# Two of six chunks of the last shared feed-forward as products of exact parts, and the last half chunk placed around the slot turns

## The chip, the cores and the metric

The kernel runs on one core of a Trainium2 chip. A core has five engines with queues of their own: TensorE (PE in the profile, its weight loads PEld), VectorE (DVE), ScalarE (ACT), GpSimd (POOL) and SyncE (SP), which issues most of the DMA transfers. [...] The metric is the device time of one execution in microseconds (us).

## What is computed

Four layers of a gated transformer: each adds a cross attention to a context and a feed-forward, both scaled by the tanh of a gate. There are 2 x 256 = 512 tokens of width 256. Only the last feed-forward matters here: a mixture of eight experts, of which each token takes two, plus a shared network that every token passes.

```python
def _shared_mlp(x_flat, shared_w_up_gate, shared_w_down):
    gu = jnp.einsum('td,dm->tm', x_flat, shared_w_up_gate)
    gate, up = jnp.split(gu, [J], axis=-1)                      # J = 704
    return jnp.einsum('tm,md->td', jax.nn.silu(gate) * up, shared_w_down)
...
logits = jnp.einsum('td,de->te', x_flat, router)                # 8 experts
topk_logits, sel = jax.lax.top_k(logits, K)                     # K = 2
...                                                             # rows go to slots of their experts
return (routed + shared).reshape(b, s, d)
```

## The kernel before

The 512 tokens stand turned in `xT` (128 rows, 2 batches, 2 halves k of the width, 256 tokens). The shared way up is done by the generator `hidden` (line 304). Its 704 columns are cut into `JCH`: chunks 0 to 4 of 128 columns, chunk 5 of 64. For each chunk two results, `pa` for the gate and `pb` for the linear half, are accumulated in PSUM over k = 0, 1, as f32 products with the weights `sh` as the stationary operand; ACT takes silu of `pa`, DVE multiplies by `pb` into `hS`. `by_batch` does chunks 0 and 1 one batch at a time (256 columns), and 2, 3 and 4 over all 512. Chunk 5 has gate and linear columns in one product (`both_w`), and with `parts=True` the generator pauses between its two products, k = 0 and k = 1. Wherever `pause(ci, b)` says so, `hidden` yields, and the caller puts other work in between.

What stands around it in the text of the last layer:

- `choose3`, `twice3`, `places` and `send3` are the routing of one half of the tokens (`halves[0]`, `halves[1]`): the two best experts, the slot numbers `goes`, and four scatters by POOL of rows into the table `xg` in HBM (helper `scatter`, line 1855). The function `between` starts the first half's routing after chunk 0; the second half's follows the first pause.
- SP reads `xg` back in five loads `xg_sb` (line 1932), once all eight scatters have landed.
- `l3_slots(g)` turns a load on PE (four transposes into a PSUM tile `tr`) and lets ACT or DVE, in alternation, copy it to `xgT`. `pair_up` is the routed way up for two groups of 128 slots, `pair_turn` turns the hidden rows (two `tr` tiles), `pair_down` goes down and scatters to `yg`. A loop over five pairs interleaves them.
- Lines 1981 to 1988 are small DVE operations on `off`, a check of the data; PE sums it over the partitions in the product `good` (line 1990).
- `kept` (lines 1913 to 1919) holds the experts' weights; POOL makes `spread` from it.

How order comes about: a scheduler places the instructions on each engine when the program is built; of those whose inputs are ready in its own model of time it takes the one that is first in the text. `inline` (line 222) chains operations by hand in the order of the text: with `pe_line` all products of this part, with `line` the DVE operations of the routing, until `line.clear()`. `behind(i, j)` puts i after j on the same engine. Once built, each engine runs its order and waits at whatever is not ready.

Buffers go round by tag: PSUM has four of `mm`, two of `tr`, two of `acc`; SBUF has eleven of `q4` and fifteen of `q2`. A tile waits for the readers of the one that held its buffer before.

The kernel has a second way to multiply, from the second layer on. `cut` (line 594) clears the low 12 bits of a float. A value is then top + low, both exact in 12 bits, and `three` (line 639) makes the product of six instructions in the type float32r: top by top and low (scaled by 2^12) by low into one PSUM tile `same`, and a third kind, of differences, into `cross`. `joined` (line 648) puts the two together: one ACT operation and one scalar_tensor_tensor on DVE.

Of the kernel before, what the change touches and what calls it, by code (L numbers as in the profile page):

```python
# [17 lines left out]
F32 = mybir.dt.float32  # L18
F32R = mybir.dt.float32r
I32 = mybir.dt.int32  # L20
U8 = mybir.dt.uint8
AF = mybir.ActivationFunctionType
ALU = mybir.AluOpType
AX = mybir.AxisListType

P = 128
NT = 4
D = 256
T = NT * P
B = 2  # L30
# [9 lines left out]
EPS = 2.0 ** -12  # L40
# [10 lines left out]
def flamingo(ctx: ExitStack, tc: tile.TileContext, a: dict, out: bass.AP):  # L51
    nc = tc.nc
# [6 lines left out]
    q4 = pool("q4", Q4)  # L59
    q2 = pool("q2", Q2)  # L60
# [7 lines left out]
    nat = pool("nat", 1)  # L68
# [35 lines left out]
    def pair(i, name, dtype=F32):  # L104
        return slab.tile([P, 2, WCOLS], dtype, tag=f"p{i}", name=name)

    def load(half, name):
        rows, cols = a[name].shape
        nc.sync.dma_start(half[0:rows, 0:cols], a[name])
        return half[0:rows, 0:cols]  # L110
# [83 lines left out]
    def behind(i, j, reason):  # L194

        tc.add_manual_dep(i.ins, j.ins.name, mybir.DependencyInfo(
            mybir.DependencyClass.NoSync, mybir.DependencyReason.DATA), reason=reason)
# [24 lines left out]
    def inline(i, line=line):  # L222
        if line:
            if line[-1] is not None:
                behind(i, line[-1], "in the order of the text")
            line[:] = [i]
        return i
# [35 lines left out]
    def batch(t, k, ts=slice(0, T)):  # L263
        return t[:, ts.start // 256 : ts.stop // 256, k, :]
# [14 lines left out]
    def mm(shape=None):  # L279
        return ps_mm.tile(shape or [P, 512], F32, tag="mm", name="mm")  # L280
# [20 lines left out]
        t = small.tile([P, 1], F32, tag="warm", name="warm", bufs=1)  # L301
        behind(nc.scalar.activation(t, eps_ln, fn), last, why)

    def hidden(xT, chunks, act_w, lin_w, hT, both_w=None, pause=lambda ci, b: False, parts=False):


        ps = {}
        for ci, (off, sz), ts in by_batch(chunks):
            if sz == 64:
                if parts:  # L310
                    p = ps_acc.tile([P, T], F32, tag="acc", name="both")
                    for k in range(2):
                        inline(nc.tensor.matmul(p, lhsT=both_w(k), rhs=batch(xT, k), start=(k == 0), stop=(k == 1)), pe_line)
                        if k == 0:
                            yield
                else:
                    p = mm()
                    chain(p, [(both_w(k), batch(xT, k)) for k in range(2)])
                s = q2.tile([P, T], F32, tag="q2", name="silu")
                nc.scalar.activation(s[64:], p[:64], AF.Silu)  # L320
                nc.vector.tensor_mul(hT[ci // 2][64:, ci % 2, :], s[64:], p[64:])
                continue
            if ci not in ps:
                ps[ci] = mm(), mm()
            pa, pb = ps[ci]
            for w, p in ((act_w, pa), (lin_w, pb)):
                chain(p[:sz, ts], [(w(k, off, sz), batch(xT, k, ts)) for k in range(2)])
            if ts.stop == T:
                s = q2.tile([P, T], F32, tag="q2", name="silu")
                silus[:] = [nc.scalar.activation(s[:sz, :], pa[:sz, :], AF.Silu)]  # L330
                nc.vector.tensor_mul(hT[ci // 2][:sz, ci % 2, :], s[:sz, :], pb[:sz, :])
            if pause(ci, ts.stop // T):
                yield
# [260 lines left out]
    def cut(dst, src):  # L594

        return nc.vector.tensor_scalar(dst.bitcast(I32), src.bitcast(I32), -4096, None, ALU.bitwise_and)
# [43 lines left out]
    def three(same, cross, left, right):  # L640

        for k in range(2):
            for i in range(2):
                inline(nc.tensor.matmul(same, lhsT=left(i, k), rhs=right(i, k), start=(k == 0 and i == 0), stop=(k == 1 and i == 1)), pe_line)  # L644
        for k in range(2):
            inline(nc.tensor.matmul(cross, lhsT=left(2, k), rhs=right(2, k), start=(k == 0), stop=(k == 1)), pe_line)  # L646

    def joined(dst, same, cross, scale=1.0):
        nc.scalar.mul(dst, cross, -EPS * scale)  # L649
        return inline(nc.vector.scalar_tensor_tensor(dst, same, (1.0 + EPS) * scale, dst, ALU.mult, ALU.add))  # L650
# [358 lines left out]
    t = totals.pop((15, 1))  # L1009
# [368 lines left out]
    def places(place, first, hot, s):  # L1378

        n = s.start  # L1380
        terms = [(s, ones_r, first[:, s]), (s, before, hot[:, s])]
        if n:
            terms += [(s, ones_r, hot[:, 0:2]), (s, ones_r, hot[:, 1:3])]
        terms += [(slice(n + 1, n + 2), ones_r, hot[:, 0:1])]
        for i, (to, lhsT, rhs) in enumerate(terms):
            inline(nc.tensor.matmul(place[:, to, :], lhsT=lhsT, rhs=rhs, start=(i == 0), stop=(i == len(terms) - 1)), pe_line)
# [269 lines left out]
    def halves_of(i, name):  # L1656
        w = pair(i, name)
        return [w[:, k, :] for k in range(2)]
# [5 lines left out]
    for q in range(QUADS + 1):  # L1664
        if q < QUADS:
            h = l2_up(q)
        if q == 0:
            second_rows()
        if 1 <= q <= QUADS:
            backs[q - 1] = l2_mask(q - 1)  # L1670
            acc = l2_down(q - 1, hTs.pop(q - 1))
            if q != 5:
                os[q - 1] = l2_halves(q - 1, acc)

        if q == 5:
            dn3 = [load(half, f"l3_dn{k}") for k, half in enumerate(halves_of(5, "dn3"))]
            sh = [load(half, f"l3_sh{k}") for k, half in enumerate(halves_of(0, "sh3"))]
            gu3 = [load(half, f"l3_gu{k}") for k, half in enumerate(halves_of(3, "gu3") + halves_of(4, "gu3"))]
        if q < QUADS:
            hTs[q] = l2_turn(q, h)  # L1680
        if q == 5:
            os[q - 1] = l2_halves(q - 1, acc)
        if 2 <= q < QUADS:
            homeward([(q - 2, 0)])
        if q == 5:
            homeward([(0, 1), (1, 1)])
        if q == QUADS:
            homeward([(4, 0), (2, 1), (3, 1), (4, 1)])
            load_table(AF.Exp, silus[0], "the table of exponentials")
# [105 lines left out]
    def l3_turned2(n):  # L1795
        tr = ps_tr.tile([P, 2, P], F32, tag="tr", name="tr")
        for k in range(2):
            inline(nc.tensor.transpose(tr[:, k, :], ext[2 * n][:, k * P : (k + 1) * P], ident), pe_line)
        nc.scalar.copy(tokens(xT, n), tr)
# [41 lines left out]
    def choose3(s):  # L1841
        for n in range(s.start, s.stop):
            inline(nc.vector.max(top[:, n, :], lgt[:, n, :]))
        inline(nc.vector.tensor_tensor(sel[:, s], lgt[:, s], wide(top[:, s, 1], 2), ALU.is_ge))

    def twice3(s):
        inline(nc.vector.tensor_tensor(hots[:, 0, s], lgt[:, s], wide(top[:, s, 0], 2), ALU.is_equal))
        inline(nc.vector.tensor_sub(hots[:, 1, s], sel[:, s].bitcast(F32), hots[:, 0, s]))
        t = small.tile([P, 2, 2], F32, tag="tie3", name="tie3", bufs=2)
        inline(nc.vector.tensor_tensor(t, top[:, s, 0:2], top[:, s, 1:3], ALU.is_equal))  # L1850
        inline(nc.vector.reduce_max(astray[:, s], t, axis=AX.X))
# [14 lines left out]
    def send3(s):  # L1866
# [10 lines left out]
                scatter(xg, goes[:, k, n : n + 1], ext[2 * n + k], E * CAP - 1, sent)  # L1877
        return i

    choose3(halves[0])  # L1880
    l3_rows(3)
    twice3(halves[0])

    def between(ci, b):
        if (ci, b) == (0, 0):
            places(place, base3, sel, halves[0])
            send3(halves[0])
            for n in (2, 3):
                l3_turned2(n)
        if (ci, b) == (1, 0):  # L1890
            for n in (2, 3):
                l3_logits(n)
        return (ci, b) in ((0, 1), (4, 1))

    shared = hidden(xT, JCH, lambda k, o, s: sh[k][:, o : o + s], lambda k, o, s: sh[k][:, 640 + o : 640 + o + s], hS,
                    lambda k: sh[k][:, 1280:], between, True)
    next(shared)
    choose3(halves[1])
    twice3(halves[1])
    places(place, base3, sel, halves[1])  # L1900
    routed = send3(halves[1])

# [5 lines left out]
    inline(nc.vector.tensor_reduce(clear3, astray, AX.X, ALU.max))  # L1908
    inline(nc.vector.tensor_scalar(clear3, clear3, -1.0, 1.0, ALU.mult, ALU.add))
    line.clear()  # L1910
    next(shared)
    kept = const.tile([P, 2, NT], F32, name="kept")
    nc.vector.tensor_scalar(w[:, 0, :], w[:, 1, :], -0.5, 0.5, ALU.mult, ALU.add)
# [89 lines left out]

    hs, hTs = {}, {}
    turn[0] = 1
    for g in range(2):
        l3_slots(g)
    next(shared)
    hs[0] = pair_up(0)
    for p in range(5):  # L2010
        if p < 4:
            hs[p + 1] = pair_up(p + 1)
        if p + 2 < 5:
            l3_slots(p + 2)
        if p == 0:
            for _ in shared:
                pass
        if 0 < p < 4:
            pair_down(p - 1)
        pair_turn(p)  # L2020
# [692 lines left out]
```

## Time and profile before

| | |
|---|---|
| median of 3 runs | 546.32 us (545.76 to 546.65) |
| the profiled execution | 545.36 us, of which the span 543.5 us |
| granted TensorE clock | 0.998 |
| PE busy | 535.0 us, 98% of the span |
| DVE, ACT, POOL busy | 61%, 44%, 23% |
| chain that ended last | PE 94%, DVE 3%, ACT 1% |
| between 485.29 and 498.25 us: PE, DVE, ACT busy | 12.96, 5.37, 2.64 us |

The span runs from the first to the last instruction of the execution; what the device time has beyond it lies around the program. Times below are counted from the span's start. A profile row names the engine, the line of the kernel, which can be a helper's (L284 is `chain`, L644 and L646 are `three`), the operation with output and input tiles, and in brackets how long the engine had stood still before and for whom. The chain of work that ended last is followed back from the last instruction: at each step to what released it, or to the one before it on its engine.

The last row is the sum of three neighbouring stretches of the shared way up, asked for one by one (485.29 to 487.85, to 491.3 and to 494.75, to 498.25): PE is full, the other engines are busy less than half of the time.

### The profile page before, as it was taken

How to read it: one execution, taken by the hardware profiler on the slowest of the kernel's cores; microseconds unless marked ns; L12 is line 12 of the kernel's file. 1: busy time of each engine (PE TensorE's matmuls, PEld its weight loads, DVE VectorE, ACT ScalarE, POOL GpSimd, SP SyncE). 2: the span in 40 equal slices, each digit the busy share in tenths (PEclk: the TensorE clock that was granted, in tenths of full speed). 3: DMA queues.
4: the chain of work that ended last, by engine and by line, in shares of the span. 5: the costliest groups of instructions: out<-in, count | busy, mean ns of one | idle time of the engine just before them, and what ended most of it. 6: DMA issues, size and time to landing. Idle time of an engine off the chain costs nothing.

```text
span 543.5 us, 8726 instructions
## 1 busy us (share of the span) xinstructions
PE 535.0 (98%) x3304; PEld 395.4 (73%) x3304; DVE 332.3 (61%) x777; ACT 238.1 (44%) x488; POOL 124.7 (23%) x229
## 2 busy tenths in 40 slices
PE   8999999999999999999999999999999999999996
PEld 6554775878888888887888888687776447884465
DVE  6999797745556454754547567765467536562322
ACT  6886466644354434444444533451433212422320
POOL 5776104111031110311012223112022001252150
PEclk9999999999999999999999999999999999999999
DMA  8910120000004000040000404599030799614013
GB/s 289 427 45 0 30 125 1 1 1 0 1 0 153 2 2 1 1 154 1 0 1 1 156 1 156 232 300 390 27 143 13 279 411 244 246 40 129 19 46 132
DMA packets 15528, 57.06 MB, mean 105 GB/s; under 512 B 2653, under 2 KB 5924, under 8 KB 12102
## 3 DMA queue, kind: packets, MB, share of 16 engines
q1 hardware_dynamic: 13718, 51.61, 25.9%
q0 software_dynamic: 1472, 4.28, 2.3%
q8 instruction: 28, 0.46, 0.3%
q10 hardware_dynamic: 288, 0.52, 0.3%
q14 instruction: 22, 0.18, 0.1%
HBM read 51.60 MB, written 5.25 MB: 105 GB/s over the span
## 4 chain that ended last, share of the span: by engine, by line
PE 94%; DVE 3%; ACT 1%; issue 0%; POOL 0%
PE mm L284 27%; PE acc L284 20%; PE mm L644 9%; PE mm L646 4%; PE mm L1590 4%; PE s L464 3%; PE acc L476 2%; PE q L644 2%; PE mm L1951 2%; PE acc L1616 2%; PE gu L644 2%; PE outT L721 1%; PE acc L1973 1%; PE q L646 1%; PE mm L1414 1%; PE y L1647 1%
## 5 line engine op out<-in xcount | busy, mean ns | idle before, releaser
L284 PE MATMUL mm<-qT,kT 128*128 128x256 f32 x256 | 60.7, 381 | 0.0
L284 PE MATMUL acc<-e,v 128*128 128x256 f32 x256 | 60.6, 379 | 0.0
L284 PEld LDWEIGHTS mm<-qT,kT 128*128 128x128 f32 x256 | 48.1, 190 | 9.2 <-ACT oT L836 1.6
L284 PEld LDWEIGHTS acc<-e,v 128*128 128x128 f32 x256 | 48.3, 189 | 8.2 <-issue 0.4
L632 POOL TENSOR_TENSOR h_parts<-w,h_top 128x256 fp32r<-128x256 f32 x28 | 20.8, 742 | 139.2 <-PE acc L284 73.6
L825 ACT ACTIVATE e<-mm 128x512 f32<-128x512 f32 x64 | 38.1, 598 | 22.3 <-PE mm L284 22.1
L828 DVE TENSOR_TENSOR t<-e,e 128x512 f32<-128x512 f32 x32 | 22.1, 691 | 23.6 <-ACT e L825 23.4
L468 ACT ACTIVATE e<-s 128x512 f32<-128x512 f32 x64 | 32.9, 605 | 5.5 <-PE s L464 5.4
L236 POOL TENSOR_TENSOR rstd<-mv,eps_ln 128x1 f32<-128x1 f32 x31 | 6.7, 217 | 108.8 <-DVE mv L235 108.8
L649 ACT ACTIVATE v<-mm 128x512 f32<-128x512 f32 x24 | 14.3, 597 | 31.1 <-PE mm L646 31.1
L644 PE MATMUL mm<-ctx_top,h_parts 128*128 128x512 f32 x56 | 27.3, 488 | 0.0
L284 PE MATMUL acc<-w,oT 128*128 128x256 f32 x112 | 26.8, 381 | 0.1
L836 ACT COPY oT<-acc 128x256 f32<-128x256 f32 x32 | 11.9, 372 | 34.2 <-PE acc L284 34.2
L650 DVE SCALAR_TENSOR_TENSOR v<-mm,v 128x512 f32<-128x512 f32 x24 | 16.6, 692 | 16.6 <-ACT v L649 16.6
L649 ACT ACTIVATE kT<-mm 128x512 f32<-128x512 f32 x28 | 16.7, 598 | 20.5 <-PE mm L646 20.5
L287 DVE SCALAR_TENSOR_TENSOR x<-acc,gsum,x 128x256 f32<-128x256 f32 x56 | 23.6, 477 | 2.8 <-PE acc L284 2.2
L650 DVE SCALAR_TENSOR_TENSOR kT<-mm,kT 128x512 f32<-128x512 f32 x28 | 19.3, 689 | 6.7 <-ACT kT L649 6.7
L284 PEld LDWEIGHTS acc<-w,oT 128*128 128x128 f32 x112 | 20.1, 190 | 3.5 <-ACT oT L836 0.5
L644 PE MATMUL mm<-v_parts,ctx_top 128*128 128x512 f32 x48 | 22.1, 461 | 0.0
L644 PE MATMUL mm<-ctx_rest,h_parts 128*128 128x512 f32 x56 | 22.0, 393 | 0.0
L464 PE MATMUL s<-w_q,ctx_nat 32*128 32x256 f32 x256 | 21.1, 400 | 0.2 <-ACT e L468 0.2
L650 DVE SCALAR_TENSOR_TENSOR qT<-q,qT 128x512 f32<-128x512 f32 x14 | 9.7, 692 | 18.4 <-ACT qT L649 18.4
(444 smaller groups left out, 1182.0 us busy)
## 6 DMA issues: line engine op xcount, KB each, us to landing
gu<-in_l_gu_all SPq DMA_DIRECT2D x14, 1024.0 KB, 7.6
w<-in_l_all SPq DMA_DIRECT2D x4, 2048.0 KB, 8.6
dn<-in_l_dn_all SPq DMA_DIRECT2D x4, 1024.0 KB, 6.2
dn<-in_l_dn_all SPq DMA_DIRECT2D x6, 512.0 KB, 9.3
gu<-in_l_gu SPq DMA_DIRECT2D x4, 704.0 KB, 18.6
ctxT<-in_ctxT SPq DMA_DIRECT2D x4, 512.0 KB, 10.9
ctx_nat<-in_ctx SPq DMA_DIRECT2D x3, 512.0 KB, 7.2
dn<-in_l_dn SPq DMA_DIRECT2D x2, 704.0 KB
```

Source lines behind the costliest of these rows:

```text
L284: inline(nc.tensor.matmul(dst, lhsT=lhsT, rhs=rhs, start=(i == 0), stop=(i == len(pairs) - 1)), pe_line)
L287: return inline(nc.vector.scalar_tensor_tensor(x[:, n, cols], acc, scalar, x[:, n, cols], ALU.mult, ALU.add))
L464: in_turn(nc.tensor.matmul(ps[j][:, k, :], lhsT=ctx_nat[rows, b, hf, c * P : (c + 1) * P], rhs=qm[rows, n, i, :], start=True, stop=True))
L468: exps.append(nc.scalar.activation(es[j], ps[j], AF.Exp))
L632: nc.gpsimd.tensor_sub(dst[1], src, t)
L644: inline(nc.tensor.matmul(same, lhsT=left(i, k), rhs=right(i, k), start=(k == 0 and i == 0), stop=(k == 1 and i == 1)), pe_line)
L646: inline(nc.tensor.matmul(cross, lhsT=left(2, k), rhs=right(2, k), start=(k == 0), stop=(k == 1)), pe_line)
L649: nc.scalar.mul(dst, cross, -EPS * scale)
L650: return inline(nc.vector.scalar_tensor_tensor(dst, same, (1.0 + EPS) * scale, dst, ALU.mult, ALU.add))
L825: nc.scalar.activation(e, s, AF.Exp)
L828: nc.vector.tensor_add(t, es[0], es[1])
L1590: inline(nc.tensor.matmul(ps[j * BLK : (j + 1) * BLK, :], lhsT=xsT[k][:, block * BLK : (block + 1) * BLK], rhs=gu2[home(q, j)][:, at : at ...
```

## The change

Chunks 3 and 4 of the shared way up are no longer f32 products. For them `hidden` calls `shared_by_parts`: for gate and linear half it runs `three` into an `mm` tile and a `tr` tile, then `joined`, then silu and the product into `hS`. The parts of the weights are made by `shared_weight_parts` (chunk 3's inside `between`, after the first half's scatters; chunk 4's after the second half's), the parts of x by `shared_x_top`, `shared_x_rest` and `shared_x_diff`, all on DVE with casts on ACT. There is one more pause, after chunk 1's second batch, and behind it the text has the parts. The parts live in buffers that held the context (`nat`, `ctxT`) and in two of `q4`. The two loads of `sh` go into one tile, by the same two transfers.

Chunk 5's first product now comes before the turns of slots 0 and 1, the second right after them; before, the first came after those turns and the second in the loop, after the turns of slots 2.

```diff
-    def hidden(xT, chunks, act_w, lin_w, hT, both_w=None, pause=lambda ci, b: False, parts=False):
+    def hidden(xT, chunks, act_w, lin_w, hT, both_w=None, pause=lambda ci, b: False, parts=False, by_parts=None, parted_chunks=()):
...
+            if ci in parted_chunks:
+                by_parts(ci, hT[ci // 2][:, ci % 2, :])
+                if pause(ci, ts.stop // T):
+                    yield
                 continue
...
-            sh = [load(half, f"l3_sh{k}") for k, half in enumerate(halves_of(0, "sh3"))]
+            sh_both = pair(0, "sh3")
+            sh = [load(sh_both[:, k, :], f"l3_sh{k}") for k in range(2)]
...
+    sx_two = nat.tile([P, 2, B, 2, 256], F32R, tag="nat", name="sx")
+    sx = [sx_two[:, 0], sx_two[:, 1], q4.tile([P, B, 2, 256], F32R, tag="q4", name="sx_diff")]
+    sw_four = turned_ctx.tile([P, 4, 2, 2, P], F32R, tag="ctxT", name="sw")
+    sw_two = q4.tile([P, 2, 2, 2, P], F32R, tag="q4", name="sw_two")
+    sw = {3: [sw_four[:, i] for i in range(3)], 4: [sw_four[:, 3], sw_two[:, 0], sw_two[:, 1]]}
+    x_tops = [q2.tile([P, 2, 256], F32, tag="q2", name="sx_top") for _ in range(B)]
+
+    def shared_weight_parts(ci):
+        w = sw[ci]
+        src = sh_both[:, :, 0:1280].rearrange("p k (j c) -> p k j c", j=2)[:, :, :, ci * P : (ci + 1) * P]
+        t = q2.tile([P, 2, 2, P], F32, tag="q2", name="sw_top")
+        inline(cut(t, src))
+        nc.scalar.copy(w[0], t)
+        inline(nc.vector.tensor_sub(w[1], src, t))
+        return lambda: inline(nc.vector.scalar_tensor_tensor(w[2], w[1].bitcast(F32), -1.0 / EPS, t, ALU.mult, ALU.add))
+
+    def shared_x_top(b):
+        i = inline(cut(x_tops[b], xT[:, b]))
+        if b:
+            behind(i, routed, "not among the routing")
+        nc.scalar.copy(sx[0][:, b], x_tops[b])
+
+    def shared_x_rest(b):
+        low = q2.tile([P, 2, 256], F32, tag="q2", name="sx_low")
+        behind(inline(nc.vector.tensor_sub(low, xT[:, b], x_tops[b])), routed, "not among the routing")
+        nc.scalar.mul(sx[1][:, b], low, 1.0 / EPS)
+
+    def shared_x_diff(b):
+        inline(nc.vector.tensor_sub(sx[2][:, b], x_tops[b], sx[1][:, b].bitcast(F32)))
+
+    def shared_by_parts(ci, dst):
+        sums = []
+        for j in range(2):
+            same, cross = mm(), ps_tr.tile([P, T], F32, tag="tr", name="cross3")
+            three(same, cross, lambda i, k: sw[ci][i][:, k, j, :], lambda i, k: batch(sx[i], k))
+            o = q2.tile([P, T], F32, tag="q2", name="shared3")
+            joined(o, same, cross)
+            sums.append(o)
+        nc.scalar.activation(sums[0], sums[0], AF.Silu)
+        nc.vector.tensor_mul(dst, sums[0], sums[1])
...
             send3(halves[0])
             for n in (2, 3):
                 l3_turned2(n)
+            shared_weight_parts(3)()
...
-        return (ci, b) in ((0, 1), (4, 1))
+        return (ci, b) in ((0, 1), (1, 1), (4, 1))
...
     twice3(halves[1])
+    shared_x_top(0)
     places(place, base3, sel, halves[1])
     routed = send3(halves[1])
...
     line.clear()
+    next(shared)
+    shared_x_rest(0)
+    shared_x_top(1)
+    shared_x_rest(1)
+    for b in range(B):
+        shared_x_diff(b)
+    shared_weight_parts(4)()
     next(shared)
...
+    next(shared)
     for g in range(2):
         l3_slots(g)
-    next(shared)
+    for _ in shared:
+        pass
     hs[0] = pair_up(0)
     for p in range(5):
...
-        if p == 0:
-            for _ in shared:
-                pass
```

More of the change, by code (lines that the diff above doesn't have):

```diff
@@ L321, in hidden @@
                 nc.vector.tensor_mul(hT[ci // 2][64:, ci % 2, :], s[64:], p[64:])
+                continue
+            if ci in parted_chunks:
+                by_parts(ci, hT[ci // 2][:, ci % 2, :])
+                if pause(ci, ts.stop // T):
+                    yield
                 continue
@@ L1892, in between @@
                 l3_logits(n)
-        return (ci, b) in ((0, 1), (4, 1))
+        return (ci, b) in ((0, 1), (1, 1), (4, 1))
     shared = hidden(xT, JCH, lambda k, o, s: sh[k][:, o : o + s], lambda k, o, s: sh[k][:, 640 + o : 640 + o + s], hS,
-                    lambda k: sh[k][:, 1280:], between, True)
+                    lambda k: sh[k][:, 1280:], between, True, shared_by_parts, (3, 4))
     next(shared)
```

## The prediction, made blind

> **What bounds the kernel now.** I read the page first: PE is busy 98% of the span at a granted clock of 0.998, and PE carries 94% of the chain that ended last. So I went to that chain for the last layer, where the change sits. Its columns are start, length (us) and what ran.
>
> ```profile
> 486.12 12.13 PE mm L284 x32
> 498.25 0.12 PE mm L1990 x2
> 498.37 0.93 PE tr L1940 x8
> 499.30 0.86 PE both L313 x2
> 500.16 4.87 PE mm L1951 x64
> 505.03 0.59 PE tr L1940 x4
> 505.62 0.86 PE both L313 x2
> 506.48 0.44 PE tr L1962 x4
> 506.92 2.50 PE mm L1951 x32
> ```
>
> Each piece starts where the one above ends: PE never pauses. The 12.13 us are the rest of chunk 1 and chunks 2, 3, 4 of the shared way up. L1990 is the small product `good`, L1940 the slot turns, the two L313 pieces the halves of chunk 5, L1951 the routed way up, L1962 its turns. The chain then stays on PE to 538.23; the gathered rows and their additions follow from the same PE products through POOL's scatters, so a shift at 500 us should reach the end whole.
>
> The price of the new kind of product is in the chain of the second layer, which already uses it:
>
> ```profile
> 113.12 0.94 PE mm L644 x4
> 114.06 0.46 PE mm L646 x2
> 114.51 1.73 PE mm L284 x8
> ```
>
> The six single-pass products of one 512-wide result take 0.94 + 0.46 = 1.40 us, most often 1.39 in this stretch.
>
> **The change, part by part.** *Chunks 3 and 4 on PE.* An f32 product is recorded as two instructions: the groups show 24 of 512 columns for the 12 products of chunks 2 to 4. The 12.13 us hold these and 8 of 256, that is 24 + 4 = 28 units of 0.433. Both outputs of a chunk take 8 units, 3.47 us. By parts: 2 x 1.39 = 2.78. Saved 0.69 a chunk, **1.37 us** for two; PE then ends chunk 4 at 496.88, if its parts are there.
>
> *The halves of chunk 5.* Work is moved, none is saved: 0.86 us go ahead of the slot turns, 0.86 from behind the third pair of slots to behind the first two. Turns start at 496.88 + 0.12 + 0.86 = 497.86. The first two slot loads are issued at 494.12 and 494.7 and land 2.7 and 2.9 us later (their rows), at 496.8 and 497.6; the second is wanted at 498.33. So they are in time by 1.0 and 0.7 us. Without the half ahead, the turns would have met them.
>
> But the half taken from 505.62 was a cover:
>
> ```profile
> 505.65 0.59 ACT L206 COPY xgT<-tr 128x512 f32<-128x512 f32 x1 [0.18 <-PE tr L1940]
> ```
>
> The third slots' turns end at 505.62 and ACT copies them out until 506.24. There are two `tr` buffers: the first hidden turn takes the free one (0.22 us), the second must wait for this copy, and so must the next way up, which reads xgT. Before, 0.86 us of chunk 5 lay there. Now the second turn can start 0.62 + about 0.05 us (478.09 to 478.13 in the chain is such a handover) after the slots' end instead of 0.22: PE stands **0.45 us**. In later turns `pair_down` (1.86 us) still covers.
>
> *Parts of chunk 3's weights.* DVE cut, subtraction, scalar_tensor_tensor, and one ACT cast. From the second layer's rows: cuts 0.42 us, subtractions 0.69, such casts on ACT 0.62. Back to back, DVE operations start closer than they last:
>
> ```profile
> 90.04 0.69 DVE L615 TENSOR_TENSOR ctx_w<-ctxT,ctx_w 128x512 f32<-128x512 f32 x1
> 90.65 0.76 DVE L596 TENSOR_SCALAR w_top<-w 128x512 int32<-128x512 int32 x2
> ```
>
> 0.61 for a 512-wide two-input operation, 0.34 for a cut. They stand in the routing's written order between 481.86 (first `goes`) and 483.87 (top of the second half), where DVE waited 2.01 us: 0.34 + 2 x 0.61 and two dependences are about 1.8. If they overrun by up to 0.9 us, PE's `places` (485.31) still hides it. Cost 0. The first half's cut of x falls into 484.89 to 485.77, also idle: 0. DVE's cost here is bounded by 0 and 0.3.
>
> *Parts of x and of chunk 4's weights* come behind the second `goes` (487.39): subtraction, cut, subtraction, two differences, then cut, subtraction, scalar_tensor_tensor: 6 x 0.61 + 2 x 0.34 = 4.3 us of DVE, plus hS of chunks 1 and 2. In the order of the text, x's parts are ready near 491.1 and the last difference near 492.0; chunk 3 starts on PE at 491.3 and wants the difference after four products, at 492.2. Chunk 4 (494.1) needs its weight parts (about 492.5) and the PSUM pair of chunk 2, which hS frees about 493.1. Slack 0.2, 0.2, 1.6 and 1.0 us: cost 0, with up to 0.5 if an operation slips in front. ACT gains 10 operations of 0.6 us in 16 us where it was mostly waiting; the four joins cost DVE 4 x 0.61.
>
> *`good` on PE* stays behind chunk 4 and needs DVE's `off` chain (L1981 to L1988), which ran until 489.98. These eight operations are last in the text. They take DVE 0.33 + 0.33 and six of 0.07, about 1.1 us, where others fill the gaps that each leaves to the next, and about 1.7 alone. Between 487.46 and 496.88, 9.4 us, DVE has 12 operations of 0.61 (hS of chunks 1 to 3, six for parts, three joins) and two cuts: 8.0 us. That leaves 1.4 us, and the joins wait for PE and ACT, so gaps are certain. I take 0; the other end is rival (b).
>
> *Joins and slot turns.* Cross results use the two `tr` buffers: the first slots' turns need the first one of chunk 4 (read by about 496.4), the second slots' the last (PE ends at 496.88, ACT reads it for 0.6: about 497.7, wanted at 498.33). ACT's copy of the first slots then stands behind chunk 4's silu and ends near 499.0; the way up wants it at 498.79 + 0.86 = 499.65, where the second half of chunk 5 hides it. Cost 0; without that half it would be some 0.3. POOL's spread moves behind a later `kept`; POOL has nothing else until 511.78.
>
> *Scatters.* The last of eight ends at 492.47 and paces the slot loads. The Trainium skill speaks against the change here (SBUF — State Buffer, Who interferes with whom): a tensor_scalar in two-port mode shuts GpSimd out for its whole length, so descriptors can't be written. The cuts (0.42 against 0.69 for the same width) look like that mode, and two fall among the last four scatters. The trace's nearest rows: scatters last 0.97 us whether or not a DVE operation runs (hS, 488.06), but none of those is a cut. By the row the loads keep their time, cost 0; by the rule, each cut delays by up to 0.42, together 0.84 against the 0.7 us of slack: PE would wait 0.14, and up to 0.7 if the first batch's two cuts delay it too. I take 0.
>
> The other edits cost nothing: one tile for `sh` instead of the same pair through a helper is the same two loads; reused context buffers were last read by 477.5. No DMA is added.
>
> **Sum.** -1.37 + 0.45 = **-0.92 us**. The profiled execution took 545.36 us (span 543.5 and 1.86 around); its sum is 544.44. It lies 0.96 below the median of the three runs, 546.32, from which I forecast **545.4**.
>
> **Rivals.** (a) *The stand at the third slots does not appear*, as the handover is hidden in the array's pipeline: the full 1.37, 545.0. For: durations of matmuls in the profile overlap by some 0.16 us; against: two separate dependences hang on the same copy.
>
> (b) *`good` becomes the new wait (slower).* The order on DVE is fixed when the program is built, by readiness and text order. If all of `off` falls behind hS of chunk 4, this is its time: the last join can't start before 497.7 (PE 496.88, ACT 0.6, handovers), so it ends at 498.4, hS at 499.1, and `off` alone takes 1.7, to 500.8. PE, which comes to `good` at 496.88, waits 3.9 us in front of everything: -0.92 + 3.9 = +3.0, 549.3, and less where a part of `off` finds a gap. For it: before, the order on DVE was already bad,
>
> ```profile
> 493.75 0.23 DVE L1919 TENSOR_SCALAR kept<-kept,tg 128x8 f32<-128x8 f32 x1 [3.77 <-POOL spread L1918]
> ```
>
> DVE stood 3.77 us behind POOL's spread, at no cost as nothing urgent was queued; now x's parts, joins and `off` can be. Two-input DVE operations beside POOL work also lengthened in the second layer (L622: 0.82 in the mean against 0.69). Against: the gaps. It eats the gain from a wait of 0.9 us on, and is a measurable loss from 2.0.
>
> (c) *The slots come late*: scatters delayed as above, or DVE late for chunk 3 by 0.5 to 1 us: the gain is used up, 546.0 to 546.4.
>
> **Chances.** The forecast 0.40, (a) 0.18, (b) 0.32, (c) 0.10. About 0.2% (1.1 us) is what a measurement of this kernel tells from no change. The forecast lies just inside; with 0.45 us of scatter in the runs half of its chance is beyond: 0.20. With (a) that is 0.38 faster. Slower: 0.28 of (b) and 0.01 of (c). The same: the rest, 0.33. The range: (a) less some scatter, 544.6, to most of (b), 548.6; the forecast's own is 544.9 to 545.9.
>
> **What would show it.** Right: 24 single-pass products at intervals of 0.23 in two blocks of 2.78; the chain free of pauses from 486 us to the third slots, then a pause near 0.45 before the second hidden turn; slot turns about 0.5 us earlier than 498.37, routed way up likewise. Wrong: a pause ahead of L1990 with DVE as releaser (b), ahead of L1940 with the DMA (c), or ahead of chunk 3's third kind of product (a late difference). If scatters last longer than 0.97 us beside a cut, the skill's rule held and not my row.

## The result, and the profile after

The changed kernel takes **547.56 us** (median of 9 runs, 547.13 to 548.52), the kernel before beside it 545.95 us (9 runs, 545.36 to 546.65): ratio **1.0031, 95% interval 1.0021 to 1.0041**. It is slower by 0.3% (1.6 us by the medians), where 545.4 us, 0.92 less than before, was forecast. The time lies inside the stated range only because that took in most of rival (b); the forecast had the direction wrong. The profiled spans are 545.3 and 543.5 us.

PE busy fell from 535.0 to 534.4 us and the row of its granted clock shows a 9 in every slice of both, so the loss is standing time. It can be placed by counting from the start of chunk 1's second batch on PE (485.98 us before, 486.24 after; this start differs by up to 1.5 us among the profiled executions below, and apart from the two loads of `sh` the first added operation starts at 482.04) to the start of the third block of the routed way up. I call this **the distance**: 20.86 us before, 508.62 - 486.24 = 22.38 after, +1.52. From there on the two traces run in step: the final products start at 526.72 and 528.50, and these 1.78 us are the 1.52 and the 0.26 by which the changed kernel's count starts later; with the spans it is 1.8.

The timeline of PE in the changed kernel; columns are start, length, what ran, and in brackets how long PE had stood before and for whom:

```profile
492.84 0.74 PE L651 MATMUL cross<-sx_diff,sw 128*128 128x512 f32 x2 [0.27 <-DVE sx_diff L1914]
...
497.12 0.63 PE L651 MATMUL cross<-sx_diff,sw_two 128*128 128x512 f32 x2
499.05 0.38 PE L2046 MATMUL mm<-off,ones 128*128 128x1 f32 x2 [1.30 <-DVE off L2044]
...
507.43 0.38 PE L2018 MATMUL tr<-ident,silu 128*88 128x128 f32 x2
508.27 0.42 PE L2018 MATMUL tr<-ident,silu 128*88 128x128 f32 x2 [0.46 <-ACT xgT L206]
508.62 2.57 PE L2007 MATMUL mm<-gu,xgT 128*32 128x352 f32 x32
```

The same places in the kernel before, without a stand:

```profile
498.09 0.28 PE L1990 MATMUL mm<-off,ones 128*128 128x1 f32 x2
...
504.96 0.66 PE L1940 MATMUL tr<-ident,xg_sb 128*128 128x128 f32 x4
...
506.84 2.57 PE L1951 MATMUL mm<-gu,xgT 128*32 128x352 f32 x32
```

Three stands, all new. The first is chunk 3 waiting for the last difference of x, the second is `good` waiting for the end of the `off` chain, the third is the second hidden turn waiting for ACT's copy of the third slots. The brackets give idle time alone; the table goes by starts, in which a stand costs more (0.66 us for the one of 0.46):

| term of the distance | us |
|---|---|
| two chunks by parts (12.11 to `good` before; 10.80 where nothing was late, in the last two experiments) | -1.31 |
| last difference late (chunk 3's second result is begun 7.18 after the start, 6.64 in the last two experiments) | +0.54 |
| `good` late (497.12 + 0.46 = 497.58 would have been its time; 499.05) | +1.47 |
| the slot turns and the halves of chunk 5 (498.09 to 504.96 and the 0.86 moved here; 499.05 to 506.94) | +0.16 |
| third slots (506.94 to 508.62, in place of 1.88 less the 0.86 moved away) | +0.66 |
| sum | +1.52 |

Why VectorE was late, in its timeline of the changed kernel:

```profile
490.62 0.57 DVE L601 TENSOR_SCALAR sw_top<-sh 128x512 int32<-128x512 int32 x1
...
491.50 0.68 DVE L1899 TENSOR_TENSOR sw_two<-sh,sw_top 128x512 fp32r<-128x512 f32 x1
492.10 0.68 DVE L1914 TENSOR_TENSOR sx_diff<-sx_top,sx 128x512 fp32r<-128x512 f32 x1
...
496.82 0.23 DVE L1975 TENSOR_SCALAR kept<-kept,tg 128x8 f32<-128x8 f32 x1 [0.43 <-POOL spread L1974]
497.25 0.69 DVE L1925 TENSOR_TENSOR hS<-shared,shared 128x512 f32<-128x512 f32 x1 [0.20 <-DVE kept L1975]
497.86 0.68 DVE L655 SCALAR_TENSOR_TENSOR shared<-mm,shared 128x512 f32<-128x512 f32 x1
498.46 0.15 DVE L2042 TENSOR_TENSOR off<-off 128x1 f32<-128x1 f32 x1
...
498.84 0.16 DVE L2044 TENSOR_TENSOR off<-off,clear 128x1 f32<-128x1 f32 x1
```

Chunk 4's weights (cut and subtraction, wanted much later) stand ahead of the difference that chunk 3 wants at once. And the last three `off` operations stand behind the scaling of `kept`, which waits for POOL, behind hS of chunk 3 and behind a join of chunk 4. In the kernel before, the last of these operations started at 489.82. VectorE did have idle time, 0.89 us of the 9.42 between 487.72 and 497.14, but not at these places of its queue.

POOL's scatters are longer too. The last four of the changed kernel:

```profile
487.93 1.31 POOL L1861 DMA_INDIRECT xg<-late,goes  x1 [0.34 <-DVE clear L1957]
489.55 1.39 POOL L1861 DMA_INDIRECT xg<-late,goes  x1 [0.30 <-issue]
491.24 0.97 POOL L1861 DMA_INDIRECT xg<-late,goes  x1 [0.30 <-issue]
492.52 1.11 POOL L1861 DMA_INDIRECT xg<-late,goes  x1 [0.31 <-issue]
```

All four took 0.97 before, the last of them:

```profile
491.50 0.97 POOL L1855 DMA_INDIRECT xg<-late,goes  x1 [0.30 <-issue]
```

They end 0.90 us later by this. The first slot load is issued at 495.42 in place of 494.12; the rest of the 1.30 us are the 0.26 of the count and 0.14 between the end of the last scatter and the load. PE did not wait for it, as it waited longer for `good`.

### The profile page after: what moved, and what is told of

Its sections match the earlier page's. It is cut to its first block, busy times and chain, and to the rows that moved or that the text cites. A ratio compares the mean times of both kernels' runs of the same rounds, so it can differ in the third digit from the quotient of the medians.

```text
span 545.3 us, 8776 instructions
## 1 busy us (share of the span) xinstructions
PE 534.4 (98%) x3312; PEld 396.2 (73%) x3312; DVE 341.6 (63%) x793; ACT 243.7 (45%) x498; POOL 125.9 (23%) x229
```

## The experiments

Theory A: the products gain what the sum says, and VectorE's queue (ahead of the crosses and of `good`) and the lost cover at the third slots cost more. Theory B: the slots come late, by the longer scatters. The runs are shown together here; their texts are below. A distance is that of the one profiled execution of its kernel, a ratio comes from 9 to 21 runs of it. Four intervals keep clear of 1: those of the changed kernel, third slots early, chunk 5 back, and the last.

| kernel | distance, us | against before | ratio to before, 95% interval |
|---|---|---|---|
| before | 20.86 | | |
| changed | 22.38 | +1.52 | 1.0031 (1.0021 to 1.0041) |
| `good` at the end | 21.12 | +0.26 | 1.0001 (0.9993 to 1.0009) |
| third slots early | 21.99 | +1.13 | 1.0023 (1.0012 to 1.0033) |
| chunk 5 back | 21.85 | +0.99 | 1.0012 (1.0006 to 1.0019) |
| chunk 5's move alone | 21.57 | +0.71 | 1.0006 (1.0000 to 1.0013) |
| chunk 4's weights early | 21.29 | +0.43 | 1.0005 (0.9996 to 1.0013) |
| the same, chunk 5 split | 20.90 | +0.04 | 1.0005 (0.9995 to 1.0014) |
| the same, x's cut early | 20.19 | -0.67 | 0.9993 (0.9985 to 1.0000) |
| the same, `kept` late | 20.42 | -0.44 | 0.9996 (0.9987 to 1.0005) |
| all mended | 20.20 | -0.66 | 0.9992 (0.9983 to 1.0002) |
| half chunk's gate last | 20.14 | -0.72 | 0.9988 (0.9979 to 0.9997) |

### `good` at the end

```diff
-    good = mm([P, D])
-    inline(nc.tensor.matmul(good[:, 0:1], lhsT=ones, rhs=off[:, 0:1], start=True, stop=True), pe_line)
...
     for p in (3, 4):
         pair_down(p)
+
+    good = mm([P, D])
+    inline(nc.tensor.matmul(good[:, 0:1], lhsT=ones, rhs=off[:, 0:1], start=True, stop=True), pe_line)
```

> The changed kernel with only the product `good` and its comparison moved behind the last pair_down; DVE's `off` chain stays where it is. Theory A (the wait of PE for `off` is the largest loss, 1.3 us idle and 1.47 by start times): PE comes to chunk 5's first product at about 497.6 instead of 499.3, the routed way up starts near 500.5 instead of 502.06, and the time falls by 1.3 to 1.5 us, from 547.56 to 546.1 to 546.3, a ratio to the kernel before of about 1.0005. Theory B (the loads of the slots, landing at 498.2 and 498.9, take its place): PE then stands in front of the slot turns and only 0.5 to 0.9 us come back. Theory C (the wait only hides DVE being late for something else, the copy of the slots): nearly nothing comes back.

Measured: 546.69 us beside 546.68, so nearly all of the loss is gone with one product moved (it no longer lies in the distance itself, which is worth 0.14 us of the 1.26 gained there). PE goes from chunk 4 to chunk 5 without a pause, and a smaller wait shows behind it, in its timeline:

```profile
497.73 1.02 PE L313 MATMUL both<-xT,sh 128*128 128x512 f32 x2
498.61 0.63 PE L1996 MATMUL tr<-ident,xg_sb 128*128 128x128 f32 x4
499.53 0.63 PE L1996 MATMUL tr<-ident,xg_sb 128*128 128x128 f32 x4 [0.29 <-DMA xg_sb<-xg]
```

So `good` was the wait (A), and the late slots (B) are real but were hidden behind it: 0.29 us once it is gone. The stands at the difference and at the third slots are unchanged (0.26 and 0.46).

### Third slots early, chunk 5 back, chunk 5's move alone

```diff
# third slots early
     for p in range(5):
+        if p == 0:
+            l3_slots(2)
         if p < 4:
             hs[p + 1] = pair_up(p + 1)
-        if p + 2 < 5:
+        if 0 < p < 3:
             l3_slots(p + 2)
# chunk 5 back
-    next(shared)
     for g in range(2):
         l3_slots(g)
-    for _ in shared:
-        pass
+    next(shared)
...
+        if p == 0:
+            for _ in shared:
+                pass
# the move alone: the kernel before, with the reverse of these lines
```

> The changed kernel with only the turns of the third slots moved ahead of the second pair of the routed way up, so that 2.4 us of products lie over ACT's copy. Theory A (the stand between the two hidden turns, 0.46 us idle and 0.66 by start times, is a loss of its own): the time falls by 0.5 to 0.7 us, to about 546.9. Theory B (PE's gaps here are made good later, since POOL's scatters and the gathered rows set the end): no change, 547.5. The third load lands near 499.9 and is wanted near 504.6, so it can't be late.

> The changed kernel with chunk 5's two products back where they were (behind the first turns, and behind the third slots' turns); chunks 3 and 4 stay in parts. If the half taken from behind the third slots is the cause of the stand there, this gives the same 0.5 to 0.7 us back as putting the slots earlier: about 546.9, with PE still 1.3 us at `good`. If the half ahead of the slot turns was needed for the loads, PE waits for them instead: with `good` ending near 499.2 and the loads landed at 498.9, I expect no such wait.

> The kernel before with only chunk 5's two products moved; all of chunks 0 to 4 are f32 products and no parts are made. Theory A: the move alone costs the stand at the third slots, 0.45 (the prediction's sum) to 0.66 us (the changed kernel's start times), 1.0008 to 1.0012 of the kernel before, and DVE is never late for `good`. Theory B (the move is free, the parts do all the harm): 1.0000. The start of the last layer's shared way up, 0.26 us later in the changed kernel's trace, should be as before if that shift comes from the parts, and anywhere within 0.3 us if it is from one execution to the next.

Measured: 547.54, 547.32 and 547.02 us beside 546.68. In the first two the stand of 0.46 at the third slots is gone and the one at `good` stays (1.30 and 1.31); the distance shrinks by 0.39 and 0.53, where 0.5 to 0.7 us was expected of each. The first of them pays some 0.1 us for each added change between turns and way up (2.50 + 0.59 + 2.50 in place of 4.87 + 0.49). The move alone, with nothing late on VectorE, has the stand of 0.46 and loses 0.71 in the distance: the lost cover is a cost of the move and has nothing to do with the parts. In the time alone (1.0006, an interval that begins at 1.0000) this would hardly be told.

### Chunk 4's weights early

The parts of chunk 4's weights depend on a load only. They are put into the attention of the last layer, where VectorE made the cut at 471.51 us.

```diff
+    shared_weight_parts(4)()
     load_table(AF.Silu, exps[-1], "the feed-forward's table")
...
     for b in range(B):
         shared_x_diff(b)
-    shared_weight_parts(4)()
```

> The changed kernel with one thing moved: DVE's three operations for chunk 4's weights stand in the attention of the last layer (DVE idle from 464.3 to 466.9 us), not behind the second half's routing; `good` stays where it is. Theory A (DVE has too much to do between 487.5 and 497 us, about 1.6 us of it these three operations and their cut): the last difference is ready before PE asks for it (0.59 us back), `off` ends before PE comes to `good` (1.47 us back), one of the lengthened scatters is short again. PE then saves its 1.37 us and pays 0.66 at the third slots: 0.5 us faster than the kernel before, 0.9990, and some 2.1 us faster than the changed kernel. Theory B (`off` comes late because it is last in the text, however full DVE is): PE still waits for about 1 us at `good`, 1.0010. Theory C (the early operations now delay the attention): the shared way up starts later by up to 1.8 us.

Measured: 546.13 us beside 545.97. Three operations out of the way, and chunk 3's crosses are on time, `good` starts with no wait at 497.90, as theory A says. But the gain in the distance, 1.09 us, is half of what was expected, since two other waits came up. PE's timeline:

```profile
497.33 0.72 PE L651 MATMUL cross<-sx_diff,sw_two 128*128 128x512 f32 x2
497.90 0.28 PE L2051 MATMUL mm<-off,ones 128*128 128x1 f32 x2
...
500.01 0.63 PE L2001 MATMUL tr<-ident,xg_sb 128*128 128x128 f32 x4 [0.43 <-ACT shared L1930]
```

The last cross (0.52 after the product ahead of it, where 0.23 is usual) waits for a PSUM buffer that ACT, behind a late join and its silu, has not yet read (it does until 497.29). For the second slots' turns the bracket names ACT's silu, which ends at 500.00, but the trace speaks for the load: it lands at 499.88, the turn's weights are already loading at 499.98, and the turn starts 0.14 us after the landing, as it does in the next kernel, where the bracket names the load (500.28 and 500.42). So theory B's late slots show here too. VectorE stood 1.50 us for POOL's `spread` at the scaling of `kept`, at 495.24, with the joins queued behind. This was the harmless stand of 3.77 us in the kernel before.

### Chunk 5 split, x's cut early, `kept` late

Three steps, each on top of the one before: chunk 5's second half goes back behind the third slots' turns (with `good` behind the second slots'); x's second cut goes ahead of the second half's scatters; the scaling of `kept` goes behind the first gate product of the experts, with `good` between the first and second slots' turns.

```diff
# split
     next(shared)
     for g in range(2):
         l3_slots(g)
-    for _ in shared:
-        pass
+    good = mm([P, D])
...
+        if p == 0:
+            for _ in shared:
+                pass
# x's cut early
     shared_x_top(0)
+    shared_x_top(1)
     places(place, base3, sel, halves[1])
# kept late (without the lines that move `good`)
-    nc.vector.tensor_scalar_mul(kept, kept, gf(3))
...
+    behind(nc.vector.tensor_scalar_mul(kept, kept, gf(3)), gated[0], "read at the end alone")
```

> As the run before, and chunk 5's second product back behind the third slots' turns (the first stays ahead of the slot turns), with `good` between the second slots' turns and the way up. The stand of 0.66 us goes; the first way up now waits for ACT's copy of the first slots with 0.12 us of `good` over it, some 0.1 to 0.3 us. Sum against the kernel before: -1.37 + 0.2, up to 0.3 for the second load: -0.9 to -1.2 us, 0.9978 to 0.9984. If instead a gap on PE here were made good by what follows, it would equal the run before, 0.9990.

> As the run before, and the cut of x's second batch ahead of the second half's scatters, so that no cut runs beside these four. If cuts lengthen scatters (0.97 us without, 1.18 to 1.39 with one), the last four take 0.97 each and the loads are issued 0.3 to 0.4 us earlier against PE; what PE waited for the second load goes, 0.0 to 0.3 us faster than the run before. If the cut only moves its harm to the first four scatters and these end later, the second batch starts up to 0.3 us later and nothing is won.

> The kernel of the last run, with the scaling of `kept`, which is read at the end alone, put behind the first gate product of the experts on VectorE, so that no join of the parts stands behind a wait for GpSimd; and with `good` between the turns of the first and of the second slots, so that the second slots' load has one product more to hide behind. Theory A (the changed kernel loses by VectorE's queue ahead of the crosses and of `good`, and by nothing that the single-pass products cost in themselves): the 1.16 us that VectorE stood goes, the wait for the second slots (0.17 us) shrinks, and the third block of the way up starts some 0.8 to 1.0 us nearer to the start of the shared way up than before the change; ratio 0.9980 to 0.9988. Rival D (the parts' own stand and the added changes of shape take the rest): the joins come sooner and nothing is won, ratio 0.9990 to 1.0000.

Measured: 546.02 and 545.35 us beside 545.97, and 545.62 beside 545.94. The first missed: with the covers gone the slots' turns waited 0.21 and 0.41 us for the loads. The second took the distance below that of before: the last cross is on time again, the loads are issued 0.5 us earlier in the count, and what is left is 0.17 us for a load. One of the last four scatters of this second kernel still took 1.29 us, beside a difference and no cut; the 1.39 that the text puts down to a cut was beside a difference, too. The third removed the stand at `kept` and gained nothing by it: PE came to the slots 0.45 us before the load. The joins were no longer what decided; of the two theories written down for it, the one that nothing is won holds, though by a load and not by the changes of shape. The 0.23 us by which its distance is worse than the second's is the load's own: in both, the last scatter ends 7.16 us after the start of the count, but the first load was issued 1.93 and 2.32 us after that end. Why is not settled; over all fourteen profiled kernels this gap lies between 1.64 and 2.36 us.

### All mended, and the half chunk's gate last

The first: x's low parts ahead of the rest on VectorE and ACT, both halves of chunk 5 and `good` ahead of the slots' turns as cover, the third slots' turns ahead of the second way up. The second: the silu and gate product of chunk 5, which only the final products read, behind the copies of the slots.

```diff
# all mended
     routed = send3(halves[1])
+    shared_x_rest(0)
...
-    next(shared)
-    l3_slots(0)
+    for _ in shared:
+        pass
     good = mm([P, D])
...
+    l3_slots(0)
     l3_slots(1)
# gate last, where the half chunk is gated
+                gate = nc.scalar.activation(s[64:], p[:64], AF.Silu), nc.vector.tensor_mul(hT[ci // 2][64:, ci % 2, :], s[64:], p[64:])
+                parts and [behind(gate[i], last_copy[i], "the slots' copies first") for i in range(2)]
```

> Every stand found so far taken away at once. The last kernel, with the low parts of x ahead of the rest of VectorE's queue and their scaling ahead of the third chunk's Silu on ScalarE (there the fourth single-pass product waited some 0.4 us for that scaling); both halves of chunk 5 and `good` ahead of the first slots' turns, as cover for their load (they waited 0.45 us there); and the third slots' turns ahead of the second block of the way up, so that no turn of hidden tiles waits for their copy. Theory A: the third block of the way up starts 0.7 to 1.0 us nearer to the start of the shared way up than before the change (0.44 us in the last kernel), less what lengthened scatters add to the slots' arrival (0.3 to 0.5 us, into the cover of 2.1 us); ratio 0.9980 to 0.9988. Rival D (a new stand takes the place of each that is removed): 0.9990 to 1.0000.

> The last kernel, with the Silu and the gate product of the half chunk (read by the final products alone) behind the copies of the first and second slots on ScalarE and VectorE, where they had held the first block of the way up for 0.30 us and a restart. Theory A: the third block starts 1.0 to 1.1 us nearer to the start of the shared way up than before the change (0.66 us in the last kernel), of the 1.3 us that the parts save TensorE; ratio 0.9978 to 0.9986. Rival D (something else is late next): 0.9988 to 0.9998.

Measured: 545.51 us beside 545.93, and 545.31 beside 546.02. Both missed the size: the distance is 0.66 and 0.72 us below that of before, where up to 1.0 and 1.1 were expected, and the ratios fall where the rivals of both texts (something else is late next) had put them. PE's timeline of the second:

```profile
500.14 1.07 PE L1997 MATMUL tr<-ident,xg_sb 128*128 128x128 f32 x8
501.45 2.57 PE L2008 MATMUL mm<-gu,xgT 128*32 128x352 f32 x32 [0.24 <-ACT xgT L206]
503.95 0.66 PE L1997 MATMUL tr<-ident,xg_sb 128*128 128x128 f32 x4
```

The way up starts 1.31 us after the slots' turns, where chunk 5's half used to lie between and the turns took 0.90: it now waits for the copy itself, and loses 0.41. A half can be cover for the load, for the first copies or for the third ones, and there are two halves. The added changes between turns and way up take 0.27 (501.45 to 507.61, in place of 6.75 less the 0.86 moved away), and the two halves side by side give 0.10 back. So 0.72 is left of the 1.31 that the parts save. Also, no wait of 0.4 us for a scaling was there to be removed: the first four products of chunk 3 show 1.49 us in both kernels, of which 0.80 is the first one's row, which overlaps the f32 product ahead of it.

The last kernel is faster than the one before by 0.03% to 0.21%. It beats the kernel before by 0.12% in the middle of that interval, less than the 0.2% that I took as the bound of what can be told, and the changed kernel by more.

### What lengthens a scatter

Two kernels measure it by itself: the kernel before, with seven operations on VectorE behind the routing whose results nothing reads, once differences of two SBUF tiles, once sums over one.

```diff
     routed = send3(halves[1])
+    spare = q2.tile([P, 2, 256], F32, tag="q2", name="spare")
+    for i in range(7):
+        behind(nc.vector.tensor_sub(spare, xT[:, 0], xT[:, 1]), routed, "not among the routing")
# or
+        behind(nc.vector.tensor_reduce(spare[:, 0, i : i + 1], xT[:, 0]..., AX.X, ALU.add), routed, "not among the routing")
```

> The kernel before, with seven differences of two tiles in SBUF (128x512, their result read by nothing) put on VectorE behind the routing's last step, so that they run while GpSimd issues the last four or five scatters of the layer. If a scatter that starts while VectorE reads two SBUF tiles is held until that operation is nearly over (in the changed kernel a scatter took 0.97 us alone, and 0.14 to 0.42 us more when 0.26 to 0.54 us of a difference was left at its start), several scatters here take 1.1 to 1.5 us, each longer by about what was left of the difference at its start less 0.12 us. If the long scatters of the changed kernel have another cause (what the matmuls or the queue did there), all stay at 0.97 us.

> The same kernel with seven sums over one tile in SBUF (128x512 in, 128x1 out) in place of the seven differences: one SBUF input each. If it is the second SBUF input that matters, the scatters beside them stay at 0.97 us; if any VectorE work on SBUF of this size does it, they lengthen as beside the differences.

Measured in one execution each (546.03 and 546.28 us beside 545.94). POOL and VectorE in the kernel with differences:

```profile
488.12 1.17 POOL L1855 DMA_INDIRECT xg<-late,goes  x1 [0.54 <-DVE goes L1873]
489.60 0.97 POOL L1855 DMA_INDIRECT xg<-late,goes  x1 [0.31 <-issue]
490.88 1.43 POOL L1855 DMA_INDIRECT xg<-late,goes  x1 [0.30 <-issue]
```

```profile
487.76 0.69 DVE L1904 TENSOR_TENSOR spare<-xT 128x512 f32<-128x512 f32 x1
...
489.17 0.68 DVE L331 TENSOR_TENSOR hS<-silu,mm 128x512 f32<-128x512 f32 x1
489.76 0.68 DVE L1904 TENSOR_TENSOR spare<-xT 128x512 f32<-128x512 f32 x1
...
490.77 0.68 DVE L1904 TENSOR_TENSOR spare<-xT 128x512 f32<-128x512 f32 x1
```

The scatter at 488.12 starts with 0.33 us of a difference left and is 0.20 longer; that at 490.88 with 0.57 left, 0.46 longer. The one at 489.60 starts inside hS (489.17 to 489.85), one of whose inputs is in PSUM, and keeps 0.97. With sums, VectorE is busy without a gap and every scatter beside it keeps 0.97:

```profile
487.95 4.24 DVE L1904 TENSOR_REDUCE spare<-xT 128x1 f32<-128x512 f32 x7
```

```profile
488.31 0.97 POOL L1855 DMA_INDIRECT xg<-late,goes  x1 [0.55 <-DVE goes L1873]
489.59 0.97 POOL L1855 DMA_INDIRECT xg<-late,goes  x1 [0.30 <-issue]
```

Fewer scatters were hit than expected (two of four), as the other two started beside hS; the size fits both times.

The cuts do it too, with one input in SBUF. None of the last four scatters of the changed kernel started during a cut, but one of the first four did, and took 1.18:

```profile
485.06 0.42 DVE L601 TENSOR_SCALAR sx_top<-xT 128x512 int32<-128x512 int32 x1
485.14 1.18 POOL L1861 DMA_INDIRECT xg<-late,goes  x1 [0.30 <-issue]
```

It starts with 0.34 us of the cut left and is 0.21 longer. With x's cut early, two of the first four start with 0.37 and 0.38 of a cut left and are 0.25 and 0.26 longer. In four other kernels the cut begins only 0.03 or 0.04 ahead of the scatter; there the scatter keeps 0.97 and the cut takes 0.49 or 0.50 in place of 0.42.

## Why the prediction was wrong, point by point

- **`good`, "I take 0".** This is the step that failed, worth 1.47 us. I compared the time that VectorE had (9.4 us) with the work it was given (8.0 us) and concluded that gaps would take in the `off` chain. The work was more than that: in the same stretch of the changed kernel (487.72 to 497.14) VectorE was busy for 8.53 us and still had hS of chunk 3 and the third join, 1.2 us, ahead of it. The two cuts took 0.45 and 0.49 us in place of 0.34, and small operations on `w` and `kept` were not in my list. And the gaps (0.26, 0.43 and 0.20 us) did not help: the order is fixed when the program is built, so an operation gets only the time at its own place, behind everything queued ahead of it. Rival (b) named the mechanism and the stand at POOL's spread that would feed it. Its price of 3.9 us was for all eight operations behind hS of chunk 4; three stood behind hS of chunk 3 and a join of chunk 4, and 1.47 was paid. That the wait was decisive is shown by the kernel with `good` at the end; with chunk 4's weights early, three operations fewer in this stretch, the chain ended at 496.20 and `good` did not wait for it. How the 1.47 us divide between the order and the amount of work is not shown: no run kept all the work and moved the `off` chain alone.
- **The last difference, "cost 0, with up to 0.5 if an operation slips in front".** One did, the subtraction of chunk 4's weights, and it cost 0.54. A slack of 0.2 us by the order of the text was no slack, as the text's order was not the engine's.
- **The third slots, 0.45 us.** Right in place, cause and row (0.46 of stand in four kernels). As a term of the sum it is 0.66: PE stood 0.46, and the starts behind it are later by 0.66. Rival (a) is out.
- **PE's saving, 1.37 us.** Measured 1.31 where nothing was late, at the intervals of 0.23 us that were named.
- **The slots.** Their loads came 1.3 us later and would have made PE wait 0.29 us without the wait at `good`; I had them in time by 0.7. I took my row (0.97 beside hS) against the rule that I read in the Trainium skill (SBUF — State Buffer, Who interferes with whom). Where a cut met the start of a scatter the rule held and not my row: 1.18 us at 485.14. That cost nothing, as the fifth scatter waited for VectorE's `clear` anyway and started no later in the count than before. Of the last four, which paced the loads, none started during a cut: that at 488.97 came while a scatter was running and was itself lengthened, to 0.53 from 0.42. What lengthened these is told by another sentence of the same section, that an instruction of VectorE with two SBUF inputs contends with a GpSimd instruction that reads SBUF. The row numbers of a scatter stand in SBUF; that it is the reading of these which contends is not shown. My row could not speak for either case, as hS has one input in PSUM. That the delay, 0.90 us, is close to the 0.84 worked out from the wrong operations is luck.
- **The sum.** -1.37 + 0.45 = -0.92 was forecast, -1.31 + 0.66 + 0.54 + 1.47 + 0.16 = +1.52 came.

What stays open is how much of the 1.31 us can be had (the best order tried kept 0.72 in the distance), and what makes the loads of the slots start sooner or later after the last scatter.

## What to carry to other kernels

A saving on the full engine is worth what the emptier engines can deliver in time, and free time there is no cover: write down the queue in front of each operation that the full engine waits for, with what each entry takes and itself waits for, the small ones too, and put the operations that nothing wants soon (here `kept`, chunk 4's weights) behind those that are wanted. A product placed between a copy and its reader may be the cover of that copy; before moving it, ask what lies there instead. Counting from a fixed point ahead of the change shows terms of some tenths of a microsecond that the start of the stage, which differs by more from run to run, would hide.

## What the runs showed of the hardware

A scatter issued by POOL that starts while VectorE runs an operation on two SBUF tiles of 128x512 f32 is longer by about what is left of that operation less 0.12 us: 0.26, 0.46 and 0.54 us left made 0.14, 0.34 and 0.42 in the changed kernel, 0.33 and 0.57 made 0.20 and 0.46 in the kernel with differences. The same holds for a cut, a tensor_scalar of that size with one SBUF input: 0.34 us left made 0.21 in the changed kernel, 0.37 and 0.38 made 0.25 and 0.26 with x's cut early. The sums, with one input in SBUF, and hS, with one of two in PSUM (0.25 us left), add nothing. The rows show it only where the operation is under way when the scatter starts: the difference that begins at 489.76, while the scatter of 489.60 runs, leaves it at 0.97.
